# A test-time-training layer with a routed feed-forward block: TensorE and VectorE issue in program-text order, the triangular substitution moves into the step that uses it, and a routed tile's two layers share one round

## The chip, the cores and the metric

One core of one Trainium2 chip. The metric is the device time of the whole program in microseconds (us), median of three runs. The engines go by the profile's names: PE is TensorE, PEld its weight loads, DVE is VectorE, ACT is ScalarE, POOL is GpSimd, SP is the queue that issues most transfers. All arithmetic that matters here is float32, and one float32 matmul of the text leaves two MATMUL records in the trace; a transpose on PE leaves one.

## The reference

Two sequences of 4096 tokens, width 512. The first layer carries a matrix W (512x512) and a bias b through the tokens of a sequence, the second is a gated mixture of eight experts:

```
K, V, Q = x @ thK.T, x @ thV.T, x @ thQ.T
for each token (k, v, q) of a sequence:
    g = 2/512 * (W @ k + b - v)
    W = W - 0.01 * outer(g, k);  b = b - 0.01 * g
    out = W @ q + b
x = layernorm(x + out)
shared  = silu(x @ sW1 + sb1) @ sW2 + sb2
act     = sqrt(softplus(x @ routing_W.T + expert_bias))        # 8 experts
combine = act, kept for the two largest of the 8
routed  = sum_e combine[:, e] * (silu(x @ rW1[e] + rb1[e]) @ rW2[e] + rb2[e])
x = layernorm(x + shared + routed)
```

## The kernel before

**Rounds.** The tokens are cut into 32 chunks of 128 tokens, and a chunk holds the tokens of both sequences (`s` = 0, 1). The token recurrence inside a chunk is turned into matrix products: the 128 error vectors of a chunk solve a triangular system, which `prep` and `join` invert. The main loop runs 32 rounds. Round c runs `step(c)`, which needs W and b as round c-1 left them; `prep(c+1)`, which doesn't; and `shared(c-1)`, the router and the shared expert of the chunk before. Each is a generator that yields a cost after a piece of work, and `interleave` always advances the one that is least far along in proportion to its total.

**Order.** Before the change the text only proposes an order: a scheduler in the build sorts the instructions of every engine by its own estimate of when they can start. Its result shows in the trace, where DVE runs 31 substitution operations without a break in the middle of the W updates.

**prep (L285 to L356).** Eight groups of matmuls make K and Q of the chunk (`pkq`, L295) and ACT copies them out (L302). `pa` (L308) makes the Gram matrices, DVE writes A1 and AQ from them (L311, L312). The four diagonal 32x32 blocks of A1 go through DRAM (`dL`, L319, four transfers, then `L`, L324, four transfers) so that DVE can invert them by substitution: 46 short operations on X (L334), 31 of which (h=0) form a chain in which each needs the one before it, while the other 15 (h=1) form a second chain. X goes through DRAM again (`dX`, L341, four transfers, then `CT`, L343), DVE transposes it (C, L347) and spreads it into D and DT (L351). All of that is done one round ahead.

**join and step (L358 to L436).** `join` multiplies M by D (`pn`, L362), ACT copies N, and three products `pz` (L370) with a DVE addition each (Z, L372) build the inverse. `step` makes `pr` for each s (L388, L393: eight matmuls, then R on DVE, L396), transposes K (`pk`, L405), then the errors (`pe`, L412, F on ACT), the outputs (`po`, L420 and L422, x on DVE, L423), four W updates (`pw`, L427, each with a DVE addition, L428), the bias update (`pb`, L432, L433) and the layernorm (L269 to L281). `pr`, `pk`, `pe`, `po`, `pw` and `pb` share three PSUM buffers.

**shared and router (L439 to L580).** Transposes `pt` (L532), router logits `pl` (L446), some 25 short DVE operations and four ACT functions with their table loads, hidden layer `ph` (L549), output `py` (L568), and the places of the chosen tokens, counted on PE (`pq`, L497) and scattered by four POOL transfers into one table in DRAM (`gt`, L515).

**Routed tiles.** The 31 chunks before the last form two groups, of 23 and 8 chunks. When a group's chunks are through, `plan` sorts its tokens by expert into tiles of 128 (99 tiles and 39), and `routed` runs them: POOL gathers a tile's tokens (`g`, L709) and its expert's weights into one of three buffers (`wb`, L715; where the buffer already holds that expert the transfer skips all its rows), PE transposes the tokens (`pg`, L724), makes the hidden layer (`phe`, L733, `he` on ACT, L737) and the output (`pye`, L744, `o` on DVE, L747), and SP writes `ge`. Tiles of the first group lie in rounds 24 to 27, those of the second after round 31. `collect` then gathers a chunk's routed rows (`z`, L783, four transfers into single buffers), adds them on DVE (L791), normalises, and writes the result: 20 chunks in rounds 28 to 31, the rest among the second group's tiles and the last chunk's experts, which `dense` computes without sorting (`pd`, L608, `pyd`, L619).

## Time and profile before

| | us |
|---|---|
| median of the runs shown (2864.4 to 2875.83) | 2871.65 |
| the profiled execution | 2863.91 |
| its span, first to last instruction | 2862.1 |
| PE busy in the span | 2664.9 (93%) |
| DVE busy | 1193.2 (42%) |
| ACT busy | 764.7 (27%) |
| POOL busy | 732.0 (26%) |

The granted PE clock is 0.978 of full speed over the span. The span less PE's busy time is what PE stood idle; matmul records overlap, so the time from the start of one record to that of the next says what a matmul costs. A wait is put down to the work that came last before it ended.

### The profile page before, as it was taken

Reading aid. Unit: us, or ns where it says so; the run is one execution under the profiler, and the core shown is the slowest. Engines: PE = TensorE matmul, PEld = TensorE weight load, DVE = VectorE, ACT = ScalarE, POOL = GpSimd, SP = SyncE. Lnnn points to the kernel's source line nnn. Section 1 sums busy time; section 2 is a strip of 40 time slices with the busy share of each in tenths; the row PEclk is TensorE's granted clock in tenths of the full one; section 3 lists DMA queues with packets and bytes.
Section 4 is the critical chain, followed back from the end, with each engine's and each line's share of the span. In section 5 each row is a group of like instructions: output and inputs, shape, how many; then the busy total and the mean of one; then the engine's idle time right before and its main releaser. Section 6 shows DMA issues by size and latency. Waiting matters only on the chain. (4 is left out here: it accounts for less than half of the span.)

```text
span 2862.1 us, 31951 instructions
## 1 busy us (share of the span) xinstructions
PE 2664.9 (93%) x10870; PEld 1731.3 (60%) x10870; DVE 1193.2 (42%) x4151; ACT 764.7 (27%) x1474; POOL 732.0 (26%) x730
## 2 busy tenths in 40 slices
PE   8999999999999999999999998999999988878886
PEld 6555566666655556666665666767666645545663
DVE  2444444444444444444444432141322477662116
ACT  1222222222222222222222222323222233335225
POOL 0011111111111111111111433243332444353333
PEclk9999999999999999999999999999999999999998
DMA  5011111111111111111111433343333377785446
GB/s 166 17 54 46 52 48 46 39 39 39 39 43 42 46 47 46 46 39 39 39 39 47 167 85 105 115 112 119 99 109 107 108 203 202 213 258 170 161 149 213
DMA packets 151635, 268.46 MB, mean 94 GB/s; under 512 B 60933, under 2 KB 61853, under 8 KB 147888
## 3 DMA queue, kind: packets, MB, share of 16 engines
q1 hardware_dynamic: 106592, 171.27, 18.8%
q0 software_dynamic: 44880, 95.15, 12.3%
q8 instruction: 86, 1.41, 0.2%
q14 instruction: 77, 0.63, 0.1%
HBM read 333.19 MB, written 87.87 MB: 147 GB/s over the span
## 5 line engine op out<-in xcount | busy, mean ns | idle before, releaser
L733 PE MATMUL phe<-gT,wb 128*128 128x128 f32 x2208 | 284.8, 284 | 55.9 <-DMA wb<-wcat_in,widx 48.9
L733 PEld LDWEIGHTS phe<-gT,wb 128*128 128x128 f32 x2208 | 272.8, 199 | 87.5 <-issue 65.7
L427 PE MATMUL pw<-F,K 128*128 128x512 f32 x512 | 248.6, 609 | 61.1 <-DVE W L428 61.1
L747 DVE TENSOR_TENSOR o<-pye,wb 128x512 f32<-128x512 f32 x138 | 95.3, 691 | 484.3 <-PE pye L744 478.6
L334 DVE SCALAR_TENSOR_TENSOR X<-L,X 128x14 f32<-128x14 f32 (+24 forms) x1472 | 282.0, 245 | 5.1
L744 PE MATMUL pye<-wb,he 128*128 128x512 f32 x552 | 264.0, 601 | 1.5 <-ACT he L737 1.5
L295 PE MATMUL pkq<-xT,thK 128*128 128x256 f32 x1024 | 238.5, 385 | 7.6 <-DMA thK<-thK_in 7.6
L388 PE MATMUL pr<-thV,xT 128*128 128x512 f32 x512 | 245.5, 604 | 0.0
L393 PE MATMUL pr<-W,kq 128*128 128x512 f32 x512 | 240.8, 596 | 0.0
L420 PE MATMUL po<-W,kq 128*128 128x512 f32 x512 | 237.1, 605 | 3.8 <-DVE W L428 3.8
L321 POOL TENSOR_TENSOR M<-A,mask 128x256 f32<-128x256 f32 x32 | 23.2, 725 | 847.3 <-DVE A L311 847.3
L295 PE MATMUL pkq<-xT,thQ 128*128 128x256 f32 x1024 | 234.7, 380 | 2.1 <-ACT kq L302 2.1
L295 PEld LDWEIGHTS pkq<-xT,thK 128*128 128x128 f32 x1024 | 194.9, 194 | 46.2 <-issue 15.8
L295 PEld LDWEIGHTS pkq<-xT,thQ 128*128 128x128 f32 x1024 | 192.6, 190 | 39.0 <-ACT kq L302 8.8
L515 POOL DMA_INDIRECT gt<-code,ri x124 | 124.4, 1003 | 329.2 <-DMA gt<-code,ri 211.9
L709 POOL DMA_INDIRECT g<-gy,gidx x138 | 139.3, 1010 | 249.8 <-PE pg L724 218.7
L715 POOL DMA_INDIRECT wb<-wcat_in,widx x138 | 138.6, 1004 | 239.7 <-issue 148.7
L427 PEld LDWEIGHTS pw<-F,K 128*128 128x128 f32 x512 | 95.0, 192 | 160.7 <-DVE W L428 70.4
L274 ACT ACTIVATE ars<-ars 128x1 f32<-128x1 f32 x64 | 12.9, 202 | 651.4 <-DVE ars L273 651.4
L428 DVE TENSOR_TENSOR W<-pw,W 128x512 f32<-128x512 f32 x256 | 175.2, 686 | 27.8 <-PE pw L427 25.0
L420 PEld LDWEIGHTS po<-W,kq 128*128 128x128 f32 x512 | 98.5, 194 | 126.5 <-issue 112.9
L783 POOL DMA_INDIRECT z<-ge,sidx x124 | 135.5, 1092 | 146.1 <-DVE acc L791 64.6
(195 smaller groups left out, 3565.7 us busy)
## 6 DMA issues: line engine op xcount, KB each, us to landing
ge<-o SPq DMA_DIRECT2D x138, 256.0 KB, 2.0
xT<-xT_in SPq DMA_DIRECT2D x32, 512.0 KB, 3.7
x<-x_in SPq DMA_DIRECT2D x32, 512.0 KB, 4.3
L<-dL SPq DMA_DIRECT2D x128, 128.0 KB, 2.8
gy<-x SPq DMA_DIRECT2D x31, 512.0 KB, 3.4
gb<-x SPq DMA_DIRECT2D x31, 512.0 KB, 3.6
acc<-gb SPq DMA_DIRECT2D x31, 512.0 KB, 4.4
y_out<-acc SPq DMA_DIRECT2D x31, 512.0 KB, 3.8
```

Of the source, the lines that this page charges most:

```text
L295: nc.tensor.matmul(ps[:, i].rearrange("p s t -> p (s t)"), th[:, dc, (ec + i) * P:(ec + i + 1) * P], xt[:, dc].rearrange("p s t -> p (s t) ...
L334: nc.vector.scalar_tensor_tensor(X[:, h, j + 1:], L[:, j + 1:, j], X[:, h, j:j + 1], X[:, h, j + 1:], ALU.mult, ALU.add)
L388: nc.tensor.matmul(ps, xt[:, dc, s, :], nthV_sb[:, dc, :], start=(dc == 0), stop=False)
L393: nc.tensor.matmul(ps, KQ[:, ec, s, 0, :], W[s][:, ec, :], start=False, stop=(ec == DC - 1))
L420: nc.tensor.matmul(ps, KQ[:, ec, s, 1, :], W[s][:, ec, :], start=(ec == 0), stop=False)
L427: nc.tensor.matmul(ps, K[s][:, ec, :], F[s], start=True, stop=True)
L428: nc.vector.tensor_tensor(W[s][:, ec, :], ps, W[s][:, ec, :], ALU.add)
L709: nc.gpsimd.indirect_dma_start(out=g_t[k], out_offset=None, in_=gr.y, in_offset=bass.IndirectOffsetOnAxis(ap=gr.gidx[:, k:k + 1], axis=0), ...
L715: nc.gpsimd.indirect_dma_start(out=wbuf[k % NW], out_offset=None, in_=wcat, in_offset=bass.IndirectOffsetOnAxis(ap=gr.widx[:, k:k + 1], ax ...
L733: nc.tensor.matmul(ps[:, hc, :], w[:, dc * HF + hc * P:dc * HF + (hc + 1) * P], t[:, dc, :], start=(dc == 0), stop=(dc == DC - 1))
L744: nc.tensor.matmul(ps, h[:, hc, :], w[:, O2 + hc * D:O2 + (hc + 1) * D], start=(hc == 0), stop=(hc == HC - 1))
L783: nc.gpsimd.indirect_dma_start(out=t, out_offset=None, in_=gr.ex, in_offset=bass.IndirectOffsetOnAxis(ap=gr.sidx[:, j, s, k:k + 1], axis=0 ...
```

## The change

PE and DVE are taken from the scheduler (`manual_schedule`): their instructions issue in the order in which the interleaved generators emit them. ACT, POOL and SP are still ordered by the scheduler. The paces of the generators are new, and `step`, `layernorm`, `router` and `collect` yield more often. `prep(c+1)` now ends with L and X's starting value; the 46 substitutions, dX, CT, C, D and DT become `invert(c)`, which runs at the start of round c itself, and `join` runs between the two halves of `pr` of s=1. M takes A1's place in memory. A routed tile's `phe`, the next tile's `pg` and the tile's `pye` stand together; `phe` of the next tile comes after, not before. Each of a chunk's four scatters has a table of its own (`gt0` to `gt3`), `plan` adds the four in PSUM, and `pq` becomes five small matmuls. `collect` fetches a chunk ahead into doubled z buffers and a third acc buffer, loads acc on POOL's queue and writes on ACT's. The hidden layers of `dense` and some constants move to other buffers to make room.

```diff
     def layernorm(t, tag, c, s, scalar=False):
...
         nc.scalar.activation(rstd, rstd, AF.Sqrt)
+        yield
         nc.vector.reciprocal(rstd, rstd)
...
-        M = prepp.tile([P, B, P], F32, tag="M", name=f"M_{c}", bufs=1)
+        M = A1
...
-        yield 2.0
+        prepared[c] = KQ, AQ, M, L, X
+
+    def invert(c):
+
+        M, L, X = prepared[c][2:]
         for j in range(SB - 1):
             for h in range(2):
                 if j >= h * HB:
                     nc.vector.scalar_tensor_tensor(X[:, h, j + 1:], L[:, j + 1:, j],
                                                    X[:, h, j:j + 1], X[:, h, j + 1:],
                                                    ALU.mult, ALU.add)
-            if j % 2 == 1:
-                yield 0.4
+            if j % 2 == 1 or j >= HB:
+                yield X_PACE
...
     def step(c):
...
                 nc.tensor.matmul(ps, xt[:, dc, s, :], nthV_sb[:, dc, :],
                                  start=(dc == 0), stop=False)
-            next(levels)
-            yield 4.5
+                if dc % 2 == 1:
+                    if s > 0:
+                        Y = next(levels)
+                    yield 2.0
...
                 nc.vector.tensor_tensor(W[s][:, ec, :], ps, W[s][:, ec, :], ALU.add)
-                if ec == 1:
-                    yield 2.0
+                yield 1.0
...
-        ps = ps_f.tile([P, 2, B, E], F32, tag="pf", name=f"pq_{c}")
-        for i, m in enumerate((before, ones16)):
+        ps = ps_f.tile([P, 2, B, E], F32, tag="pf", name=f"pq_{c}")
+        for s in range(B):
+            nc.tensor.matmul(ps[:, 0, s], before, chosen[:, s], start=True, stop=(s == 0))
...
-                    out=gr.table, out_offset=bass.IndirectOffsetOnAxis(ap=ri[:, s, k:k + 1], axis=0),
+                    out=gr.tables[s * K + k],
...
-        for k in range(-2, NT):
-            if k >= -1 and k + 4 < NT:
-                tokens(k + 4)
-            if k + 2 < NT:
-                turn(k + 2)
-                yield 0.5
-            if 0 <= k + 1 < NT:
-                hidden(k + 1)
-                yield 2.0
-            if k >= 0:
-                second(k)
-                if k + NW < NT:
-                    weights(k + NW)
-                yield 2.0
+        yield 4.5
+        turn(0)
+        yield 0.5
+        for k in range(NT):
+            if k + NW < NT:
+                tokens(k + NW)
+            hidden(k)
+            if k + 1 < NT:
+                turn(k + 1)
+            yield 2.5
+            second(k)
+            if k + NW < NT:
+                weights(k + NW)
+            yield 2.0
...
     def collect(gr):
...
+        fetch(0)
+        yield 2.0
+        for j in range(gr.n):
+            c = gr.c0 + j
+            if j + 1 < gr.n:
+                fetch(j + 1)
...
+    ctx.enter_context(tc.manual_schedule(engines={mybir.EngineType.PE, mybir.EngineType.DVE}))
+    interleave([(PREP, prep(0))])
+    interleave([(INVERT, invert(0)), (7 * KQ_PACE, part_of(ahead, 7 * KQ_PACE))])
     for c in range(NCH):
         parts = [(43.0, step(c))]
         if c + 1 < NCH:
-            parts.append((18.0, ahead) if c == 0 else (36.0, prep(c + 1)))
+            parts.append((PREP - 7 * KQ_PACE, ahead) if c == 0 else (PREP, prep(c + 1)))
         if c > 0:
-            parts.append((SHARED * (2 if c == NCH - 1 else 1), shared(c - 1)))
+            parts.append((INVERT, invert(c)))
+        if c > 0:
+            amount = SHARED + (PLAN if c in (b.c0, NCH - 1) else 0.0)
+            parts.append((amount * (2 if c == NCH - 1 else 1), shared(c - 1)))
```

Here `X_PACE` is 0.5, `KQ_PACE` 1.0, `PREP` 12, `INVERT` 95, `SHARED` 15 and `PLAN` 10.

## The prediction

> **What bounds the kernel now.** I read the busy shares first, then the busy times by stage, then PE's waits, and last the timeline around them.

> ```profile
> span 2862.1 us, 31951 instructions
> PE 2664.9 (93%) x10870; PEld 1731.3 (60%) x10870; DVE 1193.2 (42%) x4151; ACT 764.7 (27%) x1474; POOL 732.0 (26%) x730
> ```

> PE is the bound: 2862.1 - 2664.9 = 197 us are all that any order of the same matmuls can win, apart from time at a lowered clock. The stages differ (columns: stretch, its length, then busy us of PE, PEld, DVE, ACT and POOL, PEclk, DMA share, GB/s):

> ```profile
> 0.00:129.00 129.00, 112.96 (x411) 76.72 (x412) 41.72 (x176) 22.85 (x45) 11.20 (x23) 0.96 0.31 101
> 129.00:1554.00 1425.00, 1379.95 (x5059) 868.88 (x5058) 622.71 (x2398) 321.29 (x594) 217.70 (x220) 1.00 0.15 43
> 1554.00:2304.00 750.00, 715.85 (x3530) 494.58 (x3528) 241.74 (x710) 216.79 (x458) 266.96 (x264) 0.98 0.38 113
> 2304.00:2532.00 228.00, 196.37 (x652) 115.28 (x650) 172.46 (x593) 84.31 (x152) 105.74 (x97) 0.93 0.72 200
> 2532.00:2780.00 248.00, 204.31 (x1043) 141.64 (x1042) 62.83 (x137) 79.13 (x163) 95.97 (x94) 0.93 0.58 188
> 2780.00:2862.00 82.00, 55.42 (x185) 34.19 (x184) 51.77 (x138) 40.37 (x65) 34.40 (x32) 0.88 0.64 202
> ```

> Start, rounds 2 to 23, tile rounds, rounds with collect, second group's tiles, tail: PE stands idle for 16.0, 45.1, 34.2, 31.6, 43.7 and 26.6 us. What it waits for (us, times, longest):

> ```profile
> PE pw L427 <- DVE W L428: 61.1, 26, 6.0
> ...
> PE phe L733 <- DMA wb<-wcat_in,widx: 48.9, 24, 7.2
> ...
> PE pc L698 <- DMA codes<-gt,r: 10.4, 2, 9.8
> ```

> Of the first, 45.0 us are 22 waits in rounds 2 to 23, one each, about 2 us. The timeline of one shows why:

> ```profile
> 605.12 4.70 DVE L334 SCALAR_TENSOR_TENSOR X<-L,X 128x31 f32<-128x31 f32 x31
> ...
> 610.50 0.67 DVE L428 TENSOR_TENSOR W<-pw,W 128x512 f32<-128x512 f32 x1
> ...
> 611.23 1.12 PE L427 MATMUL pw<-F,K 128*128 128x512 f32 x2 [2.02 <-DVE W L428]
> ...
> 613.05 3.60 PE L388 MATMUL pr<-thV,xT 128*128 128x512 f32 x8
> ...
> 616.48 3.60 PE L393 MATMUL pr<-W,kq 128*128 128x512 f32 x8
> ```

> DVE runs 31 operations on X in one block; the W additions queue behind it, and PE finds no free PSUM buffer. The last two rows give PE's price: eight records in 616.48 - 613.05 = 3.43 us, 0.429 each, 0.858 per matmul; the 256-column ones cost 0.431 and a transpose 0.11. The starts of pr repeat every 64.55 us, of which 62.1 are matmuls at those prices, 2.3 the wait and 0.1 scattered.

> **The rounds.** The fine order puts W additions where their matmuls are, so 2.3 us per round go. The block moves into the start of the round, and what it feeds, pn, now has a deadline. Its rows from the start of the run:

> ```profile
> 43.97 4.72 DVE L334 SCALAR_TENSOR_TENSOR X<-L,X 128x31 f32<-128x31 f32 x31
> ...
> 50.98 3.90 DVE L334 SCALAR_TENSOR_TENSOR X<-L,X 128x15 f32<-128x15 f32 x15
> ...
> 58.17 0.34 SPq L343 DMA_DIRECT2D CT<-dX  x1
> ...
> 60.00 0.24 DVE L347 STREAM_TRANSPOSE C<-CT 128x64 f32<-128x64 f32 x1 [2.07 <-DMA CT<-dX]
> ...
> 60.47 0.41 DVE L351 TENSOR_TENSOR D<-C,blk 128x256 f32<-128x256 f32 x1
> ...
> 61.03 1.20 PE L362 MATMUL pn<-D,M 128*128 128x128 f32 x4 [2.96 <-DVE D L351]
> ```

> Two interleaved chains cost 4.72/31 = 0.152 us an operation; one chain by itself 3.90/15 = 0.26, for each operation needs the one before. In the new text j < 16 has 16 single operations (about 0.275, their vectors being longer: 4.4 us), then 15 pairs (30 x 0.14 to 0.152, 4.2 to 4.6). So X takes 8.6 to 9.0, longer than before.

> DVE's new order, T0 being the start of the round's first pr: brep to 0.8, layernorm of the last step in between, first X at 2.5, singles done at 7.5, pairs at 11.9 (0.9 of it layernorm). From the end of X to the issue of CT is 58.17 - 54.88 = 3.3 in the rows above and 3.4 as the median of the rounds: 15.3. CT to C 1.8: 17.1. C to pn 0.75: pn can start at T0 + 17.85.

> PE's new order ahead of pn: ten pr matmuls (8.58), twelve 256-column pkq (5.17), eight transposes pt (0.87), router logits pl (1.7): T0 + 16.35. So pn stands 1.45 us. Everything behind pn on PE waits too, as PE no longer takes other work. On DVE nothing is lost: R and the additions stand behind C, but their PSUM sources come later anyway. Later waits (pz for N and Z, pe for F, pw for W) have slack in the same walk: between two pz stand other matmuls of over 3 us, and Z costs DVE 0.7. L must land before X starts: before, the last L is issued 4.0 us after A in these rounds and lands 2.5 later, which in the new order gives T0 + 0.9, 1.6 us early. The five small pq matmuls in place of two add 0.1. New round: 62.1 + 1.45 + 0.25 = 63.8, gain 0.75, over 22 rounds and their neighbours' ends 17 us. The unknown is the stall: 0 to 3.3, so -22 to +50.

> [...]

> **Start.** 16.0 us idle, partly a load of constants (7.6) that stays; its X runs, which PE waits for at pn, b and po, now stand in a set order. 5 us (0 to 9).

> **Tile rounds.** phe waits for wb in 13 places here, 26.2 us:

> ```profile
> 1715.07 0.62 ACT L737 ACTIVATE he<-phe,wb 128x128 f32<-128x128 f32 x2 [4.39 <-PE phe L733]
> ...
> 1726.95 3.43 PE L733 MATMUL phe<-gT,wb 128*128 128x128 f32 x16 [7.24 <-DMA wb<-wcat_in,widx]
> ```

> A real load takes about 7 us from POOL's issue. A buffer comes free with pye(k) and is needed by phe(k+3). Before, phe(k+3) stood ahead of pye(k+2); now it is behind it, so the load has four records of pye (1.72) and a pg (0.44) more: 2.2 us off each wait, whose mean is 2.0. I leave 9 of 26.2. The pw wait (3.0) goes. The price: pye now follows its own he, which ends 0.99 us after phe's last record starts, with pg (0.44) and the end of phe between: 0.2 us in some 56 tiles that stand back to back, 11 us. The clock: 2% of 716 is about 14 us at half speed; fewer long waits give 3. Sum 17 + 3 + 3 - 11 = 12 (-10 to +30).

> **Collect rounds.** PE is idle 31.6: pw 13.0, the rest W, layernorm and D, all DVE (76% busy). Order cures the block behind which W stands, and doubled z and a third acc buffer take the transfer waits out of DVE's queue, where they would now block W. DVE's 172 us of 228 remain, and DMA share 0.72. I halve the idle time (16) and add 3 for the clock (0.93): 19 (0 to 40).

> **Second group's tiles.** pc's 9.8 goes: plan(b) is through before the last chunk's step ends, and its transfer lies beside it. wb 22.8 to about 10 for the reason above, other DVE and ACT waits 6.6 go, he costs 0.2 x 39 = 8, clock 4: 9.8 + 12.8 + 6.6 - 8 + 4 = 25 (5 to 45).

> **Tail.** The last chunks are collected at 9.1 us a chunk; the new order's DVE and square root per chunk come to 8.5, eight chunks: 5 (0 to 15).

> **Sum.** 5 + 17 + 12 + 19 + 25 + 5 = 83. Span 2862.1 - 83 = 2779, with the 1.8 us around it 2781, against the profiled 2863.91. That execution lies 0.27% under the median 2871.65, so in the median's terms 2781 x 2871.65 / 2863.91 = 2788.

> The clock sits under all this. It was 0.50 for 3.4 us at 491, 815 and 1269, in rounds whose only wait of note is the usual 2.3 us, and each of those rounds took 66.2 instead of 64.55. [...] I count nothing for them.

> **Rivals.**

> *Slower: the deadline of pn.* SP's queue holds dL, then the x load (512 KB, which waits for gb), then L; dX and CT stand in it too. Anything that delays L beyond its 1.6 us of slack, or CT, delays pn, and PE, in order, pays it in full in 30 rounds. Break-even is 83/30 = 2.8 us later than I walked, pn at T0 + 20.6; slower by over 0.5% from T0 + 21.1. In rounds 25 to 30 of before the last L goes out 5.2 to 8.7 us after A instead of 4.0; 8.7 everywhere is 3.1 us late. At 4 us late: 2788 + 120 = 2908. For it: PE can't fill the hole any more. Against it: in the quiet rounds (DMA share 0.15) every such distance is steady within a microsecond.

> *Ends bound by transfers and DVE.* DMA share 0.58 to 0.72 and DVE at 76% behind 2304 us: order wins nothing there. Then start and rounds alone, 22, and about 15 from the pc wait and the tiles: 2871.65 - 37 = 2835 (2832 to 2857).

> *No stall at pn.* If X starts earlier or CT is quicker, every round is PE's 62.1 + 0.25 and the whole wins 34 more; with full gains at the end, 2700 to 2745.

> **How the numbers follow.** About 0.5% (14 us) is what a measurement can tell: same is 2857 to 2886. Forecast (2745 to 2832) 0.44; no stall 0.10; ends bound 0.14; same 0.07; slower 0.25, of which some 0.09 reaches to 2905. Faster is 0.44 + 0.10 + 0.14 = 0.68. The range 2715 to 2905 leaves out 0.16 above and 0.03 below. The forecast's own range is 2745 to 2832.

> **What would show it.** Right: no pw wait for W in rounds 2 to 23, in its place pn for D, 1 to 2.5 us, and 63.8 us from round to round; wb waits of PE under 20 us in all; pc's wait gone; PE busy over 95%. Wrong: pn waits over 4 us per round; pye waiting for he over 25 us; PE idle behind 2304 us as long as before (102 us).

## The result: 4.6% slower, and the profile after

The changed kernel takes 3004.02 us (median of 4 runs, 2998.31 to 3010.17) against 2873.55 of the kernel before on the same chip: ratio 1.0461, 95% interval 1.0429 to 1.0492. The profiled execution has a span of 2996.0 us, 133.9 longer. The forecast was 2788, its range 2715 to 2905. Busy shares and the busy times by stage (same stages and columns as before, the bounds moved with the rounds; the last two are one row):

```profile
span 2996.0 us, 32353 instructions
PE 2719.3 (91%) x10977; PEld 1766.2 (59%) x10977; DVE 1292.0 (43%) x4093; ACT 811.3 (27%) x1521; POOL 763.7 (25%) x767
```

```profile
0.00:120.00 120.00, 107.28 (x404) 73.66 (x405) 43.73 (x174) 23.58 (x44) 11.24 (x23) 0.99 0.35 113
120.00:1688.00 1568.00, 1427.01 (x5141) 896.59 (x5140) 694.27 (x2355) 349.35 (x620) 220.84 (x223) 0.96 0.17 40
1688.00:2440.00 752.00, 721.42 (x3539) 501.40 (x3538) 233.82 (x671) 209.82 (x454) 265.77 (x265) 0.98 0.39 110
2440.00:2687.00 247.00, 203.91 (x673) 122.72 (x672) 180.93 (x571) 76.61 (x142) 114.07 (x110) 0.88 0.62 174
2687.00:2996.00 309.00, 259.64 (x1226) 171.79 (x1225) 139.21 (x324) 151.99 (x263) 151.75 (x147) 0.95 0.64 218
```

Cut at the first pe of a round, rounds 2 to 23 take 1568.3 us instead of 1425.4: 143.0 more, which is more than the whole difference. The other stages nearly cancel: -9.1 at the start, +1.2 in the tile rounds, +19.9 in the collect rounds, -21.1 at the end. PE's waits, and one of DVE's:

```profile
PE pn L376 <- DVE D L364: 165.6, 27, 8.5
PE pye L795 <- ACT he L788: 23.1, 27, 1.9
PE phe L784 <- DMA wb<-wcat_in,widx: 21.9, 8, 5.8
...
DVE X L347 <- DMA L<-dL: 109.0, 27, 8.9
```

The wait of pw for W is gone as forecast, and pn for D has taken its place, more than four times as long as forecast: 138.5 us in 22 rounds, 6.3 each instead of 1.45. The timeline of one round, T0 = 1073.70 (start and length in us, engine, line, operation, what ended the idle time before it; rows of other work are left out):

```profile
1065.91 1.03 POOL L550 DMA_INDIRECT gt<-code,ri  x1 [2.00 <-DVE ri L547]
...
1067.24 0.97 POOL L550 DMA_INDIRECT gt<-code,ri  x1 [0.30 <-issue]
...
1067.35 1.73 SPq L328 DMA_DIRECT2D dL<-A  x4
...
1068.51 0.97 POOL L550 DMA_INDIRECT gt<-code,ri  x1 [0.30 <-issue]
...
1069.13 0.44 SPq L145 DMA_DIRECT2D x<-x_in  x1
...
1069.79 0.97 POOL L550 DMA_INDIRECT gt<-code,ri  x1 [0.30 <-issue]
...
1069.87 2.46 SPq L333 DMA_DIRECT2D L<-dL  x4
...
1073.70 1.88 PE L401 MATMUL pr<-thV,xT 128*128 128x512 f32 x4
...
1080.51 0.56 DVE L347 SCALAR_TENSOR_TENSOR X<-L,X 128x31 f32<-128x31 f32 x2 [4.26 <-DMA L<-dL]
...
1081.65 10.06 DVE L347 SCALAR_TENSOR_TENSOR X<-L,X 128x29 f32<-128x29 f32 x44
...
1084.63 2.50 POOL L581 TENSOR_TENSOR x<-x,b 128x512 f32<-128x512 f32 x2 [8.70 <-DVE X L347]
...
1097.40 1.19 PE L376 MATMUL pn<-D,A 128*128 128x128 f32 x4 [7.12 <-DVE D L364]
```

Three things to see. X starts at T0 + 6.8, not 2.5: L's last transfer goes out by 1071.8 and lands at 1080.5. X then takes longer than forecast: two of the 44 operations last 1.12 and 1.19 us instead of 0.25, those beside the two bias additions of POOL (1084.63 to 1087.13); each of the 22 rounds has two of 1.12 to 1.31 us. And the four pr records behind this wait (1098.39) take 3.58 us, where they cost 1.88 elsewhere: the granted clock of PE is at half from 1095.0 to 1101.8. In the 22 rounds there are 21 such stretches of 3.4 to 10.2 us, mostly 6.8, 140 us in all; the kernel before has three of 3.4. In this stage of the kernel before, a load of x landed in 3.8 us and of L in 2.8 (medians); here 7.9 and 6.3.

### The profile page after: what moved, and what is told of

It reads as the page before. It is cut to its first block, busy times and chain, and to the rows that moved or that the text cites. A ratio compares the mean times of both kernels' runs of the same rounds, so it can differ in the third digit from the quotient of the medians.

```text
span 2996.0 us, 32353 instructions
## 1 busy us (share of the span) xinstructions
PE 2719.3 (91%) x10977; PEld 1766.2 (59%) x10977; DVE 1292.0 (43%) x4093; ACT 811.3 (27%) x1521; POOL 763.7 (25%) x767
## 4 chain that ended last, share of the span: by engine, by line
PE 59%; DMA 16%; DVE 14%; issue 5%; SPq 3%; ACT 2%; POOL 1%; DVEq 0%; POOLq 0%; ACTq 0%
PE pkq L304 10%; DVE X L347 9%; PE pye L795 7%; PE phe L784 6%; DMA L<-dL 6%; PE po L442 5%; PE pr L408 4%; PE pw L451 4%; PE pr L401 4%; PE ph L587 4%; DMA dL<-A 3%; PE py L608 3%; PE pa L317 3%; DMA wb<-wcat_in,widx 2%; PE pe L434 2%
## 5 line engine op out<-in xcount | busy, mean ns | idle before, releaser
L347 DVE SCALAR_TENSOR_TENSOR X<-L,X 128x31 f32<-128x31 f32 (+22 forms) x1472 | 321.7, 270 | 126.1 <-DMA L<-dL 109.0
L417 POOL TENSOR_TENSOR x<-x,brep 128x512 f32<-128x512 f32 x64 | 81.0, 1267 | 918.1 <-DVE brep L456 906.2
L784 PE MATMUL phe<-gT,wb 128*128 128x128 f32 x2208 | 276.3, 279 | 23.3 <-DMA wb<-wcat_in,widx 21.9
L795 PE MATMUL pye<-wb,he 128*128 128x512 f32 x552 | 268.5, 609 | 24.3 <-ACT he L788 23.1
L401 PE MATMUL pr<-thV,xT 128*128 128x512 f32 x512 | 284.7, 685 | 0.0
L304 PE MATMUL pkq<-xT,thK 128*128 128x256 f32 x1024 | 245.7, 384 | 7.5 <-DMA thK<-thK_in 7.5
L788 ACT ACTIVATE he<-phe,wb 128x128 f32<-128x128 f32 x276 | 86.5, 363 | 435.8 <-PE phe L784 434.7
L311 ACT COPY kq<-pkq 128x256 f32<-128x256 f32 x256 | 84.6, 373 | 433.6 <-PE pkq L304 433.6
L376 PE MATMUL pn<-D,A 128*128 128x128 f32 x128 | 33.8, 411 | 165.6 <-DVE D L364 165.6
L447 DVE TENSOR_TENSOR x<-po,x 128x512 f32<-128x512 f32 x64 | 44.2, 691 | 316.8 <-PE po L446 316.8
L795 PEld LDWEIGHTS pye<-wb,he 128*128 128x128 f32 x552 | 98.5, 191 | 125.9 <-issue 78.9
```

The source lines that it names most:

```text
L304: nc.tensor.matmul(ps[:, i].rearrange("p s t -> p (s t)"), th[:, dc, (ec + i) * P:(ec + i + 1) * P], xt[:, dc].rearrange("p s t -> p (s t) ...
L347: nc.vector.scalar_tensor_tensor(X[:, h, j + 1:], L[:, j + 1:, j], X[:, h, j:j + 1], X[:, h, j + 1:], ALU.mult, ALU.add)
L401: nc.tensor.matmul(ps, xt[:, dc, s, :], nthV_sb[:, dc, :], start=(dc == 0), stop=False)
L784: nc.tensor.matmul(ps[:, hc, :], w[:, dc * HF + hc * P:dc * HF + (hc + 1) * P], t[:, dc, :], start=(dc == 0), stop=(dc == DC - 1))
L795: nc.tensor.matmul(ps, h[:, hc, :], w[:, O2 + hc * D:O2 + (hc + 1) * D], start=(hc == 0), stop=(hc == HC - 1))
```

## The experiments

Times are medians of the runs; "rounds" is the time of rounds 2 to 23. The medians of the kernel before, run beside each set, lay between 2857.8 and 2870.1, so times of different sets can differ by some 12 us for that reason alone; the ratios given are to the kernel before of the same set. Each edit is made to the changed kernel, and the diffs are abridged.

**E1, SP in text order**
```diff
-engines={PE, DVE}
+engines={PE, DVE, SP}
```

> SP's queue, too, keeps the order of the text, so that the x load (512 KB) comes behind the four L loads instead of ahead of them. Theory Q (L waits behind x in SP's queue): the last L lands about 3 us after its issue instead of 6 to 9, X starts some 4 us earlier, PE's wait at pn falls from 7.1 to about 3 us per round and most of the half-clock windows after it go (1.6 us per round): a steady round 65 to 67 us instead of 71.3, the whole 2850 to 2890. Rival D (L is slow because its own DRAM reads are slow at that point, or the deadline is missed by the in-order chain itself): L still lands after 6 us or more, the round stays within 1 us of 71.3, the whole 2975 to 3010.

2949.17. The pn wait goes (6.2 us in all), but the load of xT, now behind L and gb (the store of a chunk's sum) in SP's order, takes its place:
```profile
PE pkq L304 <- DMA xT<-xT_in: 128.4, 29, 10.4
```
Unclear by itself: pkq stands ahead of pn and hides D's time.

**E2, x on ACT's queue**
```diff
-nc.sync.dma_start(out=x_t[c], ...)
+(nc.sync if c < 2 else nc.scalar).dma_start(out=x_t[c], ...)
```

> The x load is issued on ACT's queue instead of SP's; all else as changed. Theory Q in its narrow form (the descriptors of one queue are worked off in order): L lands 3 to 4 us after issue, as with x behind it, round 65 to 67 us, whole 2850 to 2890. Rival E (the two transfers share the 16 DMA engines whatever their queue): L still takes 6 us or more beside x, round 70 us or more, whole above 2960.

3007.57, pn waits 168.3 us: no change. In one round L even waited to be issued (1086.48, where dL went out at 1081.57), since dL's small writes were late too: POOL waited for them until 1090.17. From 200 to 1500 us X waits for L 67.5 us (18 times) with x on ACT's queue, 64.0 (18 times) with x on SP's. So it isn't the order within one queue.

**E3, no bias addition on POOL**
```diff
-nc.gpsimd.tensor_tensor(y[:, s, :], y[:, s, :], b2_sb, ALU.add)
```

> Leaves out the addition of the shared expert's second bias on POOL (two 128x512 operations of 1.25 us per round), so the output lacks that bias. Theory P (an X operation that falls beside a POOL tensor operation takes 1.1 to 1.2 us instead of 0.25): the two long X operations go, X is 1.9 us shorter, PE's wait at pn falls from 7.1 to about 5.2 us, round 69.4, whole 2945 to 2960. Rival: the long operations have another cause (a late operand, the L tail); they stay, and the time stays within 15 us of 3004.

2909.38, nearly twice the gain expected. X's block is 9.4 us instead of 11.2 and holds no long operation any more, and the pn waits fall from 165.6 to 99.2 us over the run. Two things weren't counted: X also starts 0.7 us earlier (T0 + 5.6), for which no run shows the reason, and shorter waits mean less time at half clock (PE is busy 1410.8 us in rounds 2 to 23 instead of 1427.0). POOL's two additions cost each operation of X that stands beside one 0.9 us (11.2 less 9.4 for the two); by what means, no run shows.

**E4 and E7, the substitution one round ahead again, in text order**
```diff
         prepared[c] = KQ, AQ, M, L, X
+        yield L_PACE
+        yield from invert(c)
...
-            parts.append((INVERT, invert(c)))
```
The paces are set anew in both; E7 leaves more text between the transfers and what needs them.

> Undoes the move alone: the substitution, its DMAs, C, D and DT go back to the end of prep, one round ahead, still in fine text order on PE and DVE; everything else as changed. Theory M (the move with its deadline is the loss, the order is a gain): no wait at pn in rounds 2 to 23, no wait at pw, a round 62.6 to 63.6 us, whole 2790 to 2835. Rival O (text order itself costs): the pn wait goes but waits of 3 us or more per round come up elsewhere (DVE standing at L or C with W additions behind it), round above 66, whole above 2870.

> The substitution one round ahead as in the fourth run, but with more work between its two transfers and the operations that wait for them (A to X 8 us of text, X to C 6 us), still text order on PE and DVE. Theory S (text order is good if the text leaves each transfer its time; the fourth run lost because DVE stood at C for CT, 3.5 us a round, with W additions behind it): no wait at pn, pw waits under 1 us per round, a round 62.6 to 64 us, whole 2795 to 2835. Rival O (text order costs in itself): pw or other waits of over 3 us per round stay, whole above 2880.

2998.31 and 3042.04, both misses. pn no longer waits, but pw does (E4: 88.0 us behind x, 61.9 behind W; E7: 131.6 and 42.4): X stands in DVE's text order ahead of the x and W additions of the second sequence, as the block did in the kernel before. In one round of E4, X runs from 1054.71 without a wait for L, the x addition comes behind its first 16 operations (1059.25), and PE waits 2.5 us for it. More text between the transfers (E7) moved X deeper among the additions. Neither place of the move alone is what costs; both orders put X in front of something that PE needs.

**E5, x behind L, xT ahead of dL; E6, also the bias on DVE**
```diff
+engines={PE, DVE, SP}; load_xT(c + 2) after the second pr
-nc.gpsimd.tensor_tensor(y[:, s, :], y[:, s, :], b2_sb, ALU.add)     # E6
+nc.vector.tensor_tensor(y[:, s, :], y[:, s, :], b2_sb, ALU.add)     # E6, after ph
```

> SP in text order as in the first run, and the xT load, whose lateness took the place of the wait, is now issued ahead of dL; the x load stays behind L. Theory Q+P (x ahead of L costs 4.3 us, two X operations beside POOL's bias addition 1.9): X starts at T0 + 2.5, pn comes at about T0 + 19.7, PE waits some 3 us there instead of 7.1, a round 65.5 to 67 us, whole 2870 to 2905. Rival (the first run's gain came from somewhere else than L): pn still waits over 5.5 us, whole above 2940.

> The run before, with the shared expert's second bias added on DVE after the hidden layer (two operations of 0.69 us) instead of on POOL beside X. Theory Q+P: X 1.9 us shorter, pn at T0 + 17.9, PE waits 1 to 2 us, no half-clock windows in most rounds, a round 63.8 to 64.6 us, whole 2815 to 2850, below the kernel before. Rival (C and CT, not L and POOL, set the deadline): pn waits over 3 us, whole above 2870.

2948.60 and 2873.53. With x out of the way L still lands only 5.5 us after issue, and X starts at T0 + 4.6 instead of 6.3 (2.5 was forecast): x ahead of L is less than half of L's delay. The bias on DVE is worth 75 us here.

**E8, PE and DVE left to the scheduler**
```diff
-ctx.enter_context(tc.manual_schedule(engines={PE, DVE}))
```

> The changed text, but PE and DVE are left to the scheduler again. Theory M (the moved substitution is the loss, whoever orders): PE waits for D or for W additions over 3 us per round, whole 2900 to 2990. Rival O (text order is the loss): the scheduler fills the hole at pn with other matmuls, a round under 65 us, whole below 2860.

2780.86, ratio 0.9699 (0.9671 to 0.9727): the rival holds. Rounds 1374.9, PE without any wait. One round, T0 = 1021.14:
```profile
1021.14 1.88 PE L401 MATMUL pr<-thV,xT 128*128 128x512 f32 x4
...
1035.76 3.68 PE L401 MATMUL pr<-thV,xT 128*128 128x512 f32 x8
...
1039.28 1.89 PE L304 MATMUL pkq<-xT,thK 128*128 128x256 f32 x8
...
1041.01 1.89 PE L587 MATMUL ph<-yT,w 128*128 128x256 f32 x8
...
1042.73 1.88 PE L408 MATMUL pr<-W,kq 128*128 128x512 f32 x4
...
1044.45 0.61 PE L376 MATMUL pn<-D,A 128*128 128x128 f32 x4
```
pn stands at T0 + 23.3, no earlier than in the changed kernel (23.7 in the round shown), and D is done only at 23.05 (median). But PE has 6 to 7 us of other matmuls ahead of it. D isn't late for the same reason, though: X starts at T0 + 2.4 and ends at 13.5, and the time goes between X and C (CT is issued 5.4 us after X's end, 3.0 in the changed kernel). X is early because in this run x lands in 3.9 us and L in 3.7, in the same queue order: its last scatter is issued by 1003.5, eleven us before dL (1014.8). That gave the next theory.

**E9, the scatters earlier; E16, no scatters**
```diff
+            if s == 0:
+                next(routing, None)      # ahead of the first py
...
-            if s == B - 1:
-                next(routing, None)      # behind the last py
```

> The changed kernel with one line moved: the router's last DVE operations, and with them POOL's four scatters gt, stand ahead of the first py instead of behind the last, some 10 us earlier in the round; SP's queue keeps x between dL and L. Theory G (what slows x and L is the scatters, which in text order go out in the same 6 us as dL, x and L; under the scheduler they are done 10 us before, and the same queue order lands x in 3.9 and L in 3.7 us): x lands in about 4 us instead of 7.9, L in about 4 instead of 6.3 (median), X starts 3 to 4 us earlier, PE waits 3 to 4 us at pn instead of 7.1, a round 66 to 68 us instead of 71.3, whole 2880 to 2920. Rival Q (x ahead of L in SP's queue is enough by itself): x and L land as late as before, whole above 2975.

E16 leaves the four scatters out and moves nothing:

> The changed kernel without the four scatters of a chunk, all else in its place, so the tables stay zero and every routed row is taken from token 0. Theory G (the scatters themselves are what slows dL, x and L): X starts at about T0 + 2.5 as with the scatters early, PE waits 3 to 4 us at pn, rounds 2 to 23 take 1450 to 1475 us instead of 1568, whole 2850 to 2885. Rival (the router's DVE operations, which moved with the scatters, were what counted): rounds 2 to 23 stay above 1540, whole above 2960.

2869.99 (ratio 1.0015) and 2856.15 (0.9945); rounds 1466.9 and 1462.7. In both X starts at T0 + 2.47 (median). dL goes out 6.35 us ahead of T0 in E9 as in the changed kernel, so A is no earlier; E16 shows that it is the scatters, not the DVE operations that moved with them. The moved line is worth 134 us (4.5% by the ratios). In E16 the last L lands at T0 + 1.9, in the changed kernel at 6.0 (medians of the landings that the trace has): some 1.8 us of that is a later issue, since L waits for dL, and the rest is L's own time to landing, 6.3 instead of 4.1.

**E15, one table again**
```diff
-out=gr.tables[s * K + k],
+out=gr.tables[0],
```

> The changed kernel with the four scatters going to one table again, so that each waits for the one before; place in the round, queue order and all else as changed. Theory B (the burst: four scatters 1.3 us apart are what slows dL, x and L): spaced by 3 us or more they let x land in 4 to 5 us and L in 3 to 5, a round 66 to 69 us, whole 2880 to 2950. Rival L (their late place is enough): x lands after 6 us or more, L after 5.5 or more, the whole 2980 to 3015.

3016.95. x lands in 5.0 us and L in 5.3, and X starts at T0 + 4.2 and no longer at 6.3, so the burst is part of the delay; but spaced by 3 to 7 us the scatters, and POOL's work behind them, reach into X's own time: in one round an X operation lasts 1.95 us beside a scatter and the x addition that follows it, and pn is as late (T0 + 22.8, median). The late place is enough for the loss, though not by L's landing alone, as the rival had it.

**E10, E9 and the bias on DVE**

> The run before, and the bias addition on DVE instead of POOL. If G and P (POOL's lock) are the two terms that the forecast missed, pn comes at about T0 + 18 as forecast, PE waits 1 to 2.5 us there, a round 63.7 to 65 us, the whole 2815 to 2850. If something else delays D too, pn waits above 3 us and the whole stays above 2870.

2798.45, ratio 0.9761 (0.9726 to 0.9796); rounds 1398.8. The same rows (POOL's first scatter of the four, 1.3 us apart):
```profile
1016.41 1.03 POOL L550 DMA_INDIRECT gt<-code,ri  x1 [29.30 <-DVE ri L547]
...
1031.33 2.46 SPq L333 DMA_DIRECT2D L<-dL  x4
...
1035.38 1.88 PE L401 MATMUL pr<-thV,xT 128*128 128x512 f32 x4
...
1037.84 0.56 DVE L347 SCALAR_TENSOR_TENSOR X<-L,X 128x31 f32<-128x31 f32 x2
...
1038.97 8.23 DVE L347 SCALAR_TENSOR_TENSOR X<-L,X 128x29 f32<-128x29 f32 x44
...
1052.89 0.68 PE L376 MATMUL pn<-D,A 128*128 128x128 f32 x4 [0.93 <-DVE D L364]
```
The forecast walk put the first X at T0 + 2.5, its end at 11.9, pn at 17.85 and PE's wait at 1.45. Here they are 2.46, 11.8, 17.5 and 0.93. P is the theory of E3; no run shows a lock, only that two of X's operations last longer beside POOL's two additions.

**E11, join later; E14, the same on E10**
```diff
-Y = next(levels)       # behind matmuls 2, 4, 6, 8 of the second pr
+Y = next(levels)       # behind 6, twice behind 8, behind pk
```

> The changed kernel with join later in the text: pn behind the sixth matmul of the second pr instead of the second, the last pz behind pk. D comes as late as in the changed kernel. Theory J (the loss is what PE has ahead of pn in text order, not the lateness of D, which the scheduler's run has too: pn at T0 + 23.3 there without a wait): PE works 5 to 7 us more ahead of pn, waits 0 to 2 us there and about 1 us in all at pz, a round 64 to 66 us, whole 2830 to 2870. Rival: what the late join moves stands in pz, pe or F instead (over 4 us a round), whole above 2930.

> Text order with gt early, bias on DVE and join late. Theory: the mended kernel stands 1.0 us per round at pn, and the late join brought 1.8 us of pz and pe waits with it; so together a round comes to 63.4 to 64.4 us and the whole to 2790 to 2820, no gain: once D keeps its time, work put ahead of pn buys nothing. Rival: the two waits are independent of D's time and the pn wait of 1.0 goes, rounds 62.6, whole 2770 to 2785.

2845.60 (ratio 0.9926) and 2803.12 (0.9761, as E10). join's pieces stand behind single matmuls of the second pr, not in one place between its halves as the section on the change has it, so they can be moved one by one. With D as late as ever, work ahead of pn wins 158 us (5.4% by the ratios; rounds 1428); with D in time it wins nothing, for pz (14.1 us in 21 rounds) and pe (11.4) wait instead.

**E12, scheduler up to round 27; E13, text order in rounds 28 to 31 alone, with E10's edits**

> A candidate: scheduler up to round 27, text order on PE and DVE from round 28 on. In the collect rounds text order took 247 us, the scheduler with the same text 264; in the last stage 309 and 293. If the stages add up: 2781 less 17 plus 16, within 15 us of 2780; if what the scheduler put ahead across the border is lost, up to 2800.

> A candidate: the changed text, scheduler on PE and DVE except in the four collect rounds, which keep text order; gt ahead of py; bias on DVE. If the stages add up from the runs so far (119 to the end of round 1, 1375 for rounds 2 to 23, 720 tile rounds, 235 collect rounds as in the mended kernel, 293 at the end as under the scheduler): 2742, within 15 us. If what the scheduler put across the borders is lost, 2765 to 2785, no better than the scheduler alone.

2781.56, which is 0.9702 of before and no better than E8, and 2764.51, 0.9623 of before (0.9591 to 0.9655), the fastest seen. Its stages came within 6 us of the sum but the last, which takes 313.8 us where the scheduler alone had 293.4.

## Why the prediction was wrong

| median over rounds, after T0 | X starts | X ends | pn |
|---|---|---|---|
| forecast | 2.5 | 11.9 | 17.85 |
| changed | 6.3 | 17.5 | 23.1 |
| E9, scatters early | 2.5 | 13.9 | 19.5 |
| E10, and bias on DVE | 2.5 | 11.8 | 17.4 |

- **The step that failed** is "L ... lands 2.5 later, which in the new order gives T0 + 0.9, 1.6 us early". That duration was measured where next to nothing stood beside L: in a round of before L went out from 596.40 on, the first scatter at 599.66, x at 613.30. The text order moves the router's last DVE operations, and with them POOL's scatters, into the 6 us of dL, x and L, and L lands at T0 + 6.0 (see E16). The prediction followed SP's queue past L, but not POOL's, and it named only one late neighbour (x). E5 and E16 show x to be the lesser: with x alone beside it L lands at T0 + 1.9, still 0.6 us before X needs it, instead of the 1.6 that the walk had.
- **X's length**, "8.6 to 9.0", was right by itself (E10: 9.4 with the layernorm in between) and lacked the time that POOL's additions cost, 2.1 us (E9 against E10). The kernel before already showed it: an X operation lasts 0.72 us instead of 0.22 and ends with POOL's addition.

```profile
614.22 1.27 POOL L398 TENSOR_TENSOR x<-x,brep 128x512 f32<-128x512 f32 x1 [2.90 <-DVE brep L433]
...
614.79 0.72 DVE L334 SCALAR_TENSOR_TENSOR X<-L,X 128x9 f32<-128x9 f32 x1
```

- **C to pn**, 0.75 in the walk, is 1.03 in the walk's own rows (60.00 to 61.03) and 0.86 in E10; it changes little.
- **The clock.** I counted no half speed for the new wait. PE is busy 1427.0 us in these rounds and 1379.5 in E10 with the same matmuls: 47.5 us. That is the clock's share: in the 140 us at half clock PE works for 95.5 us, and half of that, 47.8, is what the lower clock adds. With the waits (138.5 against 19.5) that makes 166.5 of the 169.5 us between the two in these rounds. The prediction's times of half clock in the kernel before were some 10 us late: the granted clock falls at 480.6, 804.9 and 1258.9. At 480.6 the 3.4 us ahead of it hold 1.37 us of PE's work, the usual wait being wholly inside (columns as in the tables of stages):

```profile
477.20:480.60 3.40, 1.37 (x7) 0.66 (x6) 3.40 (x18) 0.00 (x0) 0.99 (x1) 1.00 0.01 3
480.60:484.00 3.40, 3.40 (x5) 1.34 (x6) 2.24 (x6) 0.00 (x0) 0.00 (x0) 0.50 0.39 151
```

So there the usual wait of 2.03 us was followed by half clock; the forecast counted nothing for that, and nothing for the waits of 6.3 us that came in its place.
- **The slower rival** had the mechanism (pn's deadline, paid by PE in order) and its price per us; I priced it at 4 us late and gave it 0.25. pn came 5.3 us late, and the time at half clock came on top.
- **"On DVE nothing is lost"** and "PE can't fill the hole" were the two sides of one choice. E8 shows what the hole is worth: with D as late, the scheduler's PE order loses nothing. That its 2781 lies so near the forecast of 2788 is chance: its rounds gain 50 us and not 17, its collect rounds lose 37 instead of gaining 19.
- **X's operations**, one by one, were priced about right: from start to start they come 0.29 us apart as singles and 0.14 in pairs in E10's rounds, where the rows of before had 0.26 and 0.152.
- **Tile rounds**, forecast -12, came to +1.2. phe's wait for wb fell from 26.2 to 14.2 there, pye's for he is 7.7 (forecast 11). In E9 the stage takes 731.4 and in E16 728.6, so the late scatters cost here too.
- **Collect rounds**, forecast -19, came to +19.9: pn, with two waits of over 8 us, then pt and pz. E10 leaves 234.6 against 227.3 before; three waits of X for L (18.5 us) remain. E16 takes 228.3, which points to the scatters here too, but there every tile gathers the same token, so it isn't quite the same work. Whether z's gathers or acc's loads delay L was not tried.
- **The end**, forecast -30 for both parts, gave -21.1; the start -9.1 instead of -5.

## What to carry to other kernels

When an order is written by hand, a short chain through DRAM becomes a deadline, and every transfer that the new order puts beside it counts, from whichever queue it is issued: here L, on SP's queue, took 6.3 us beside POOL's four scatters and 4.1 without them (E16). Take the landing time from a place with the same neighbours, or move the neighbours. A wait of an in-order PE can cost more than its length: here 138.5 us of waits brought 140 us at half clock, 47.8 us more. So it pays to put independent matmuls ahead of a wait like that, which is what the scheduler did (E8, no wait in rounds 2 to 23) and the late join (E11, 158 us).
